# Attention of layer 0: three small matmuls per pair of rows trade places and one of them changes its PSUM bank

## The chip, the cores and the metric

The kernel runs on one core of one Trainium2 chip. The metric is the device time of one execution in microseconds (us). The engines are TensorE (PE in the profile), VectorE (DVE), ScalarE (ACT), GpSimd (POOL) and SyncE (SP, which only issues DMAs here).

## The reference, cut to what matters

The program has two layers on a picture of 256 x 256 positions with 128 channels. Layer 0, which the change touches, is an attention within each row of the picture, ahead of a residual addition:

```
xn = layernorm(groupnorm(x));  tri_bias = xn @ w_tri          # one bias per head, [h, m, n]
q = xn @ w_q / sqrt(32);  k = xn @ w_k;  v = xn @ w_v         # 4 heads of 32 channels
for each row i of 256:                                        # 256 positions m, n in a row
    scores = q[i] @ k[i].T + tri_bias + mask_bias[i, n]
    o[i] = softmax(scores over n) @ v[i]
x = x + (sigmoid(xn @ w_g + b_g) * o) @ w_o + b_o
```

Layer 1 is a convolution and a selective scan over windows in four directions, and takes about nine tenths of the time. The change doesn't touch it.

## The kernel before, in words

Channels lie on the 128 partitions and positions on the free axis. A first part normalises x and stores xn in HBM. Then the attention of layer 0 runs over 256 rows, two rows being a *pair* of 512 positions (class `Pair`, class `Row`). The order of all instructions is written out by hand (`tc.manual_schedule()`, the loop over `s` at L567): each engine carries out its own instructions in the order in which this loop issues them, and waits where its data or its buffer isn't ready. Layer 1 follows, with an order of its own.

One *step* s of the loop takes one row, and four rows are under way at once:

- `now` is row s: its scores in PSUM get their bias (`add`, L472, VectorE), their maximum (`peak`, L480, VectorE) and their exponential (`exps`, L488, ScalarE). That is done in two halves of two heads each.
- `nxt` is row s+1: `scores` (L462, TensorE).
- `mid` is row s-2: `turn` transposes its exponentials on TensorE (L516); `turn_out` copies them out of PSUM, one half on VectorE (L528), the other on ScalarE (L530).
- `old` is row s-3: `mix` multiplies with the values into `o_p` (L539, TensorE).
- At the end of a step the sums of row s-1 are inverted (L498, VectorE) and spread (`widen`, L503, GpSimd); GpSimd also prepares the bias of row s+2 (L449).

What is done once for a pair is spread over its two steps, s even and s odd. `ahead` is the next pair, `behind` the previous one, `done` the one before that:

- for `ahead`: `queries` (L364) and `queries_out` (L368), `keys` (L372) and `keys_out` (L376), `values` (L381) and `values_out` (L391); the matmuls are TensorE's, the copies out of PSUM ScalarE's;
- for `behind`: `gates` (L395, TensorE), `gates_out` (L399, VectorE) and the sigmoid in three passes of ScalarE (`logistic`, L131 to L133); `shares`, the transposes of the inverted sums (L409, TensorE), and `shares_out`, which multiplies them into the gate (L416, VectorE);
- for `done`: `gather`, gate times mixed values (L420, VectorE); `project`, the output projection (L424, TensorE); `project_out`, bias and residual (L427, VectorE); `store`, statistics for the next group norm (L432, VectorE) and the DMA to HBM (L433, SP).

PSUM has eight banks, and all of them are in use: four hold the scores, two the transposed exponentials (`aT_p`), one, `ps_o`, holds `o_p`, and one, the side bank (`side0`, tag "m"), is used by `g_p`, `q_p`, `y_p`, `k_p`, `rd_p` and `v_p` in this turn, once each in a pair. Each of the six has to wait until the one ahead of it has been read out.

The order within a step, with what stands in even or odd steps alone:

```
even: mix, add 0, peak 0, turn 0, exps(1 of 4), gather, turn_out 0, exps(3 of 4), gates, gates_out,
      add 1, turn 1, turn_out 1, peak 1, queries, queries_out, exps(4), scores, project,
      sigmoid, invert, widen
odd:  mix, add 0, peak 0, turn 0, exps(1 of 4), project_out, turn_out 0, exps(3 of 4), keys, keys_out,
      add 1, turn 1, turn_out 1, peak 1, shares, shares_out, exps(4), scores, values, values_out,
      store, invert, widen
```

Of the kernel before, what the change touches and what calls it, by code (L numbers as in the profile page):

```python
# [12 lines left out]
F32 = mybir.dt.float32  # L13
# [6 lines left out]
P = 128  # L20
# [47 lines left out]
def kernel(  # L68
# [60 lines left out]
    def logistic(e):  # L129

        nc.scalar.activation(e, e, AF.Exp, scale=-1.0)  # L131
        nc.scalar.activation(e, e, AF.Ln, bias=one)
        nc.scalar.activation(e, e, AF.Exp, scale=-1.0)  # L133
# [42 lines left out]
    for dh in range(2):  # L176
        for k in range(KD):
            o, back = k % 2, k // 2
# [82 lines left out]
    with tc.tile_pool(name="lnc", bufs=1) as cp, tc.tile_pool(  # L261
        name="lnx", bufs=3
    ) as xp, tc.tile_pool(name="lnt", bufs=3) as tp, tc.tile_pool(
        name="lnp", bufs=2, space=PSUM
# [47 lines left out]
    with tc.tile_pool(name="atc", bufs=1) as cp, tc.tile_pool(  # L312
        name="atx", bufs=7
    ) as xp, tc.tile_pool(name="att", bufs=3) as tp, tc.tile_pool(
        name="ats", bufs=8
    ) as wp, tc.tile_pool(name="atps", bufs=1, space=PSUM) as ps_s, tc.tile_pool(
        name="atpt", bufs=1, space=PSUM
    ) as ps_t, tc.tile_pool(name="atpm", bufs=1, space=PSUM) as ps_m, tc.tile_pool(
        name="atpo", bufs=1, space=PSUM
# [17 lines left out]
        def side0(name):  # L337
            return ps_m.tile([P, 512], F32, name=name, tag="m")

        class Pair:  # L340
# [79 lines left out]
                nc.vector.tensor_mul(self.og, self.o_p, self.gate)  # L420

            def project(self):
                self.y_p = side0("y_p")
                nc.tensor.matmul(self.y_p, wo, self.og, start=True, stop=True)  # L424

            def project_out(self):
# [8 lines left out]
        class Row:  # L435
# [96 lines left out]
            def mix(self):  # L532
                pair = self.pair
                if self.r == 0:
                    pair.o_p = ps_o.tile([P, 512], F32, name="o_p")
                for n in range(2):
                    for h in range(NH):
                        base = h * HC
                        nc.tensor.matmul(  # L539
                            pair.o_p[base : base + HC, self.row],  # L540
                            pair.vs[:, self.r, n, base : base + HC],
                            self.aT[h][:, n, :],
                            start=(n == 0),
                            stop=(n == 1),
                        )
# [4 lines left out]
        def pick(items, i):  # L550
            return items[i] if 0 <= i < len(items) else None

        with tc.manual_schedule():
            for pair in pairs[0:4]:
                pair.load()
            first = pairs[0]
            first.mask_bias()
            rows[0].bias()
            rows[1].bias()
            first.queries()  # L560
            first.queries_out()
            first.keys()
            first.keys_out()
            rows[0].scores()
            first.values()
            first.values_out()
            for s in range(n_rows + 4):  # L567
                sg, odd = divmod(s, 2)
                now, nxt, mid, old = (
                    pick(rows, s),  # L570
                    pick(rows, s + 1),
                    pick(rows, s - 2),
                    pick(rows, s - 3),
                )
                ahead, behind, done = (
                    pick(pairs, sg + 1),
                    pick(pairs, sg - 1),
                    pick(pairs, sg - 2),
                )
                if not odd:  # L580
                    if sg + 4 < n_pairs:
                        pairs[sg + 4].load()
                    if behind:
                        behind.load_residual()
                    if ahead:
                        ahead.mask_bias()
                if s + 2 < n_rows:
                    rows[s + 2].bias()
                if old:
                    old.mix()  # L590
                if now:
                    now.add(0)
                    now.peak(0)
                if mid:
                    mid.turn(0)
                if now:
                    now.exps(0, [0])
                if done:
                    if odd:
                        done.project_out()  # L600
                    else:
                        done.gather()
                if mid:
                    mid.turn_out(0)
                if now:
                    now.exps(0, [1, 2, 3])
                if odd and ahead:
                    ahead.keys()
                    ahead.keys_out()
                if not odd and behind:  # L610
                    behind.gates()
                    behind.gates_out()
                if now:
                    now.add(1)
                if mid:
                    mid.turn(1)
                    mid.turn_out(1)
                if now:
                    now.peak(1)
                if odd and behind:  # L620
                    behind.shares()
                    behind.shares_out()
                if not odd and ahead:
                    ahead.queries()
                    ahead.queries_out()
                if now:
                    now.exps(1, [0, 1, 2, 3])
                if nxt:
                    nxt.scores()
                if odd and ahead:  # L630
                    ahead.values()
                    ahead.values_out()
                if not odd and done:
                    done.project()
                if odd and done:
                    done.store()
                if not odd and behind:
                    logistic(behind.gate)
                if 0 <= s - 1 < n_rows:
                    rows[s - 1].invert()  # L640
                    rows[s - 1].widen()
# [778 lines left out]
```

## Time and profile before

| what | value |
|---|---|
| median of 3 runs (lowest, highest) | 24756.14 us (24755.36, 24756.92) |
| the profiled execution, and its span | 24756.32 us, 24754.5 us |
| mean granted TensorE clock in the whole span | 0.987 of full speed |
| attention of layer 0: first and last start of L472 | 543.3 us, 2720.6 us |
| busy in those 2177.3 us: PE, DVE, ACT, POOL | 1870.3, 1925.2, 1729.2, 1334.9 us |
| mean granted TensorE clock in them | 0.96 |

The profile gives, for each engine, the time in which it was busy with an instruction; the rest is waiting, and the trace says for each wait which instruction of which engine ended it. The matmuls' ends are modelled, and records of neighbouring instructions on one engine overlap a little, so the distance from one start to the next is shorter than the duration of a record. All numbers of the trace are from the one profiled execution.

### The profile page before, as it was taken

The page shows a single profiled execution, that of the slowest core. Times are in us where ns is not written, and L with a number is a line of the kernel's source. Part 1 is how long each engine was busy: PE and PEld are TensorE (multiplying, and loading weights), DVE is VectorE, ACT ScalarE, POOL GpSimd, SP SyncE. Part 2 cuts the span into 40 slices and gives each one's busy share as a digit, 9 for nine tenths or more (in the row PEclk, how much of TensorE's full clock was granted, in tenths as well). Part 3 has the DMA queues.
Part 4 walks back from the last instruction along what each step waited for, and adds up shares of the span by engine and source line. Part 5 has one row for each costly group of instructions (what it writes and reads, how often), then busy time and mean ns, then how long its engine had stood idle before and what let it go on. Part 6 is the DMA issues. An engine that isn't in the chain of part 4 may idle for free.

```text
span 24754.5 us, 429436 instructions
## 1 busy us (share of the span) xinstructions
PE 23738.4 (96%) x171020; PEld 17003.5 (69%) x171020; DVE 22137.9 (89%) x14740; ACT 18874.1 (76%) x35334; POOL 21878.7 (88%) x10062
## 2 busy tenths in 40 slices
PE   7888899999999999999999999999999999999999
PEld 2555577777777777777777777777777777777776
DVE  6888899999999999999999999999999999999998
ACT  5777777777777777777777777777777777777776
POOL 3666699999999999999999999999999999999999
PEclk9999999999999999999999999999999999999999
DMA  5222344444444444444444444444444444444444
GB/s 192 63 63 62 101 155 156 156 153 155 155 155 154 152 155 156 156 155 152 155 155 155 155 154 154 156 156 154 153 154 156 155 154 155 153 155 156 155 154 143
DMA packets 2000343, 3638.88 MB, mean 147 GB/s; under 512 B 1129584, under 2 KB 1131760, under 8 KB 1725824
## 3 DMA queue, kind: packets, MB, share of 16 engines
q1 hardware_dynamic: 1985616, 3602.35, 43.1%
q8 instruction: 1346, 22.05, 0.4%
q10 hardware_dynamic: 12720, 9.07, 0.1%
q14 instruction: 661, 5.41, 0.1%
HBM read 3467.33 MB, written 143.65 MB: 146 GB/s over the span
## 4 chain that ended last, share of the span: by engine, by line
PE 82%; DVE 8%; ACT 6%; issue 2%; POOL 1%; DMA 0%; ACTq 0%; SPq 0%; DVEq 0%; POOLq 0%
PE b_p L1173 31%; PE y_p L1206 28%; DVE h L1189 5%; PE cv_p L762 5%; PE dt_p L1011 4%; ACT at L488 2%; PE xd_p L942 2%; PE dut_p L1045 2%; PE in_p L717 1%; PE o_p L878 1%; PE y_p L1064 1%; PE z_p L796 1%; PE u_p L915 1%; PE sc L462 1%; POOL h L1195 1%
## 5 line engine op out<-in xcount | busy, mean ns | idle before, releaser
L1195 POOL TENSOR_TENSOR h<-h,cc 128x1024 f32<-128x1024 f32 x8192 | 19182.8, 2369 | 1524.1 <-DVE h L1189 1514.1
L1189 DVE TENSOR_TENSOR_SCAN h<-da,b_p 128x1024 f32<-128x1024 f32 x8192 | 18346.7, 2274 | 2068.7 <-PE b_p L1173 2011.5
L1160 ACT ACTIVATE da<-dt,am 128x508 f32<-128x508 f32 x16384 | 10663.9, 708 | 1910.4 <-DVE h L1189 1899.3
L1173 PE MATMUL b_p<-diag,dut 64*128 64x256 f32 x65536 | 9139.4, 401 | 388.2 <-DVE h L1189 386.8
L1206 PE MATMUL y_p<-ident,h 128*128 128x128 f32 x65536 | 8168.1, 278 | 7.7 <-POOL h L1195 7.6
L1206 PEld LDWEIGHTS y_p<-ident,h 128*128 128x128 f32 x65536 | 7207.2, 142 | 1406.7 <-issue 1062.0
L1173 PEld LDWEIGHTS b_p<-diag,dut 64*128 64x128 f32 x65536 | 5700.1, 186 | 3303.5 <-issue 1848.3
L734 ACT ACTIVATE tap<-xin,wtap 128x512 f32<-128x512 f32 x2048 | 1519.6, 742 | 0.5
L762 PE MATMUL cv_p<-ident,tap 128*128 128x128 f32 x9216 | 1446.1, 280 | 31.1 <-ACT tap L734 27.1
L1021 ACT ACTIVATE sp<-dt_p 128x512 f32<-128x512 f32 x1024 | 610.3, 596 | 1079.2 <-PE dt_p L1011 1078.4
L1034 POOL TENSOR_TENSOR du<-dt,u 128x512 f32<-128x512 f32 x1024 | 1308.6, 1278 | 59.9 <-DMA z<-bt 57.0
L762 PEld LDWEIGHTS cv_p<-ident,tap 128*128 128x128 f32 x9216 | 1037.9, 141 | 390.4 <-issue 204.9
L1151 ACT ACTIVATE da<-ident 128x16 f32<-128x16 f32 x1536 | 349.3, 227 | 1202.2 <-DVE h L1189 1202.1
L488 ACT ACTIVATE at<-at,nmax 128x256 f32<-128x256 f32 x2048 | 1019.2, 501 | 240.0 <-DVE nmax L480 240.0
L449 POOL TENSOR_TENSOR tm<-trib,mb 128x2048 f32<-128x2048 f32 x256 | 1166.3, 4556 | 10.7
L1011 PE MATMUL dt_p<-xd,wdt 9*128 9x512 f32 x2048 | 1149.6, 641 | 2.5 <-DVE dt L1027 2.2
L503 POOL COPY wide<-rden 128x256 f32<-128x256 f32 x256 | 101.6, 397 | 828.5 <-DVE rden L498 826.6
L1054 ACT COPY dut<-dut_p 128x512 f32<-128x512 f32 x1024 | 589.0, 575 | 256.9 <-PE dut_p L1045 245.2
L1022 ACT ACTIVATE sp<-sp,one 128x512 f32<-128x512 f32 x1024 | 739.6, 722 | 33.7
L1027 DVE SCALAR_TENSOR_TENSOR dt<-sp,dt_p 128x512 f32<-128x512 f32 x1024 | 677.9, 662 | 15.4 <-DMA z<-bt 11.5
L516 PEld LDWEIGHTS aT_p<-ident,at 128*128 128x128 f32 x4096 | 450.8, 141 | 343.0 <-issue 142.6
L472 DVE TENSOR_TENSOR at<-sc,tm 128x1024 f32<-128x1024 f32 x512 | 614.4, 1200 | 57.7 <-POOL wide L503 30.3
(132 smaller groups left out, 16405.1 us busy)
## 6 DMA issues: line engine op xcount, KB each, us to landing
cc<-c_d SPq DMA_DIRECT2D x2048, 1024.0 KB
diag<-z SPq DMA_DIRECT2D x1024, 1024.0 KB
xt<-in_x_dram SPq DMA_DIRECT2D x16, 2048.0 KB
xt<-in_x_dram SPq DMA_DIRECT2D x32, 1024.0 KB
xn_d<-xn SPq DMA_DIRECT2D x32, 1024.0 KB
xn<-xn_d SPq DMA_DIRECT2D x128, 256.0 KB
mb<-in_mask_dram SPq DMA_DIRECT2D x128, 256.0 KB
xr<-in_x_dram SPq DMA_DIRECT2D x128, 256.0 KB
```

The lines of the kernel that those rows point to most:

```text
L449: nc.gpsimd.tensor_add(self.tm, trib.rearrange("p h m n -> p (h m) n"), self.pair.mb[:, self.row].unsqueeze(1).to_broadcast([P, 2 * NH, IMG]),
L488: nc.scalar.activation(self.at[hp][:, j, :], self.at[hp][:, j, :], AF.Exp, bias=self.nmax[hp][:, j : j + 1], accum_out=self.den[:, 2 * hp ...
L734: nc.scalar.activation(scaled.rearrange("p s (y x) -> p s y x", x=WIN), self.xin[:, dh] .rearrange("p y f x -> p (y f) x")[:, 2 * dy : 2 * ...
L762: nc.tensor.matmul(cv_p[:, s], now[:, s], ident, start=(tap == 0 and s == 0), stop=(tap == 8 and s == GS - 1), is_transpose=True, skip_gro ...
L1011: nc.tensor.matmul(token_order(self.dt_p), wdt[rows, self.o, dh * P : (dh + 1) * P], token_blocks(self.xd[rows]), start=True, stop=True,)
L1022: nc.scalar.activation(sp, sp, AF.Ln, bias=one)
L1034: nc.gpsimd.tensor_mul(token_blocks(du), token_order(self.dt[back][dh]), token_blocks(self.u[:, dh]),)
L1160: nc.scalar.activation(da[:, :, j, lo:hi], dt[:, :, lo:hi], AF.Exp, scale=am[:, a0 : a0 + 1])
L1173: nc.tensor.matmul(b_p[:, s, :, h * 64 : (h + 1) * 64].rearrange("p n t -> p t n"), job.dut[self.back][rows, p, h, self.dh * P : (self.dh ...
L1189: nc.vector.tensor_tensor_scan(out=out_, data0=d0, data1=d1, initial=0.0, op0=ALU.mult, op1=ALU.add)
L1195: nc.gpsimd.tensor_mul(self.h, self.h, cc.rearrange("p n s t -> p s n t"))
L1206: nc.tensor.matmul(job.y_p[:, 2 * p + s, self.dh * P : (self.dh + 1) * P], self.h[:, s, j], ident, start=(first and s == 0 and j == 0), st ...
```

## The change

Three things change in the order, and one buffer. The projection's result `y_p` is written into the bank of `o_p` instead of the side bank, and `project` with `project_out` stands in the even step behind `queries_out`; before, `project` was at the end of the even step and `project_out` in the odd one. `keys` and `keys_out` stand at the end of the even step, behind the scores and ahead of the sigmoid; before, they were in the odd step ahead of `add 1`. The matmuls of `shares` take the place of the keys in the odd step, ahead of the second turn and of the values; `shares_out` stays. The turn of the side bank becomes `g_p`, `q_p`, `k_p`, `rd_p`, `v_p`.

```diff
             def project(self):
-                self.y_p = side0("y_p")
+
+                self.y_p = ps_o.tile([P, 512], F32, name="y_p", tag="o")
                 nc.tensor.matmul(self.y_p, wo, self.og, start=True, stop=True)
...
             def mix(self):
                 pair = self.pair
                 if self.r == 0:
-                    pair.o_p = ps_o.tile([P, 512], F32, name="o_p")
+                    pair.o_p = ps_o.tile([P, 512], F32, name="o_p", tag="o")
...
                 if now:
                     now.exps(0, [0])
-                if done:
-                    if odd:
-                        done.project_out()
-                    else:
-                        done.gather()
+                if done and not odd:
+                    done.gather()
                 if mid:
                     mid.turn_out(0)
                 if now:
                     now.exps(0, [1, 2, 3])
-                if odd and ahead:
-                    ahead.keys()
-                    ahead.keys_out()
+                if odd and behind:
+                    behind.shares()
                 if not odd and behind:
                     behind.gates()
                     behind.gates_out()
...
                 if now:
                     now.peak(1)
                 if odd and behind:
-                    behind.shares()
                     behind.shares_out()
                 if not odd and ahead:
                     ahead.queries()
                     ahead.queries_out()
+                if not odd and done:
+                    done.project()
+                    done.project_out()
                 if now:
                     now.exps(1, [0, 1, 2, 3])
...
                 if odd and ahead:
                     ahead.values()
                     ahead.values_out()
-                if not odd and done:
-                    done.project()
+                if not odd and ahead:
+                    ahead.keys()
+                    ahead.keys_out()
                 if odd and done:
                     done.store()
```

## The prediction, made before the result was known

> **What bounds the kernel now.** I read the page first: one core, 24754.5 us of span inside an execution of 24756.3. The edit touches only the attention of layer 0, so I cut that stage out: the first score addition (L472) starts at 543.3 us, the last at 2720.6. Those are 255 steps (one image row each), 8.54 us a step, **17.08 us a pair of rows**. Then the view by windows, first over the steady part, then over two single pairs (from the L472 that opens an even step to the next such):
>
> ```profile
> core 0: us, PE busy (x) PEld busy (x) DVE busy (x) ACT busy (x) POOL busy (x), PEclk, DMA share, GB/s
> 700.00:2700.00 2000.00, 1721.32 (x13597) 1032.85 (x13596) 1773.05 (x2227) 1591.90 (x4921) 1227.22 (x586) 0.96 0.21 62
> ...
> 1514.98:1531.42 16.44, 14.03 (x118) 8.34 (x117) 15.05 (x20) 13.55 (x43) 10.48 (x5) 1.00 0.19 66
> ```
>
> No engine is full, VectorE (DVE) comes nearest with 89%, and it does the same 15.05 us of work in a pair of 16.44. So I asked what DVE, TensorE (PE) and ScalarE wait for (columns: total us, times, longest):
>
> ```profile
> DVE gate L416 <- PE rd_p L409: 155.2, 117, 1.6
> DVE at L472 <- POOL wide L503: 28.4, 45, 1.0
> DVE gate L399 <- PE g_p L395: 26.9, 48, 0.6
> ...
> PE rd_p L409 <- ACT ks L376: 162.8, 117, 1.4
> PE k_p L372 <- DVE xr L427: 72.9, 117, 0.6
> PE aT_p L516 <- ACT aT L530: 39.7, 117, 0.3
> ```
>
> One wait stands out and comes once in each of the 117 pairs: DVE's product with the shares waits for the transposes rd_p, and these wait for ScalarE's copy of the keys, because k_p and rd_p use the one side bank in turn. k_p in turn waited for DVE to empty y_p out of that bank. The chain of waits over one pair shows what it hangs on:
>
> ```profile
> 1522.29 2.08 ACT at L488 x8
> 1524.37 0.53 ACT gate L131
> ...
> 1526.31 0.49 ACT at L488 x2
> 1526.81 0.47 ACT aT L530
> 1527.28 1.49 ACT at L488 x6
> 1528.77 0.48 ACT ks L376
> 1529.24 0.14 issue
> 1529.38 0.63 PE rd_p L409 x4
> 1530.01 1.08 PE sc L462 x16
> ```
>
> ScalarE runs exponentials and the sigmoid without a gap, the keys' copy is last in that row, and everything on PE and DVE stands behind it. Last, the granted clock in two odd steps:
>
> ```profile
> 1494.00:1496.00 2.00, 1.07 (x8) 0.79 0.81 221
> 1496.00:1498.00 2.00, 2.00 (x17) 0.50 0.02 8
> ...
> 1528.00:1530.00 2.00, 0.62 (x8) 1.00 0.66 235
> ```
>
> (after the PE busy time: clock, DMA share, GB/s.) PE is nearly idle for that wait, and in some pairs the clock then falls to 0.50 for about 4 us: scores take 2.09 us there instead of 1.15, and the next L472 and L399 wait (the 45 and 48 cases above, some 40% of 117). A pair without a drop takes 16.44, the mean is 17.08: the drop costs **0.64 us a pair** on average.
>
> **What the Trainium skill says.** "TensorE: Matmul & The Clock Gate", Part 1, says that an idle window of about 3.4 us takes the array to half its clock and a busy one restores it, the windows running freely. The trace agrees in kind: 0.50 after a gap, only in some pairs. The worst 3.4 us of the fast pair (1525.98 to 1529.39) still hold 1.67 us of PE work, 49%, so a half-idle window seems to be enough here. "PSUM — Partial Sum Buffer", Engine vs sequencer instructions: ScalarE, VectorE and GpSimd take their queues strictly in order and matmuls complete in program order. The trace agrees: k_p was computed by 1526.4, yet its copy starts at 1528.66, after the exponentials issued ahead of it. The same page, PSUM bank collisions, asks that a bank be guarded as a whole: y_p in the bank of o_p must wait for gather (L420) to have read o_p, which its data need anyway.
>
> **The change part by part.** I lay out one pair from t=0 at the even step's first L472 (1514.98 in the trace), with start-to-start distances from there: L472 1.21 and 1.14, peak L480 1.14, gather 0.60, turn copy 0.60, gates 0.67, L427 0.66, shares product 0.61, statistics 0.60, reciprocal 0.10. Counts per pair 4, 4, 1, 4, 1, 1, 1, 1, 2: that is 15.00 us without waits. Taken from the other side, 16.44 less 1.36 for L416's gap and 0.12 for L399's is **14.96 us**, which I use.
>
> *Removed on DVE:* the wait before L416. Work removed or added: none on any engine; every matmul and copy stays, they change places.
>
> *Even step, DVE:* L472 0, peak 1.21, gather 2.35, copy 2.95, gates 3.55 to 3.67, L472 4.34, copy 5.47, peak 6.07, then the moved project_out (L427) at 7.19, reciprocal 7.85, end 7.96. *PE:* mix 0.68, turn 1.68, gates 2.6, second turn 3.68 (after DVE's copy), queries 4.61, **project 5.57 to 6.62** (1.05), scores to 7.71, keys 8.68 (0.97). Project waits for gather, over at 3.0: nothing. project_out wants y_p at 6.7 and comes at 7.19: slack 0.5, cost nothing. The scores are 1.05 later behind project, but the next L472 is 0.66 later too: 7.71 against 7.96. *ScalarE:* queries_out ends at 6.2, so the side bank is free long before keys; exponentials 7.31 to 9.29 (behind the peak), keys_out to 9.77 (k_p was ready at 8.7), sigmoid to 11.72. In front of the sigmoid keys_out delays it by 0.48; gone from the odd step it gives that back. The sigmoid's result is wanted by the shares product at 13.8, 2 us later.
>
> *Odd step, PE:* mix at 8.68 takes the o bank, free since project_out ended near 7.93; turn to 10.61; **shares at once**, since keys_out freed the bank at 9.8 and GpSimd's wide copy comes some 0.6 after the reciprocal (8.6): 10.61 to 11.17, 3 us ahead of their use. Second turn: first half to 11.75; second half waits for ScalarE's L530, 0.96 after the sigmoid (12.68), to 13.4. Scores 14.5, values 14.55. *DVE:* L472 7.96, peak 9.17, copy 10.31, L472 10.91, copy 12.06 (its transposes end at 11.8), peak 12.66, shares product 13.8, statistics, reciprocal, end **15.0**. Values wait for that product (14.49): nothing. The next gates reach DVE near 18.55, DVE stands there at 18.5 to 18.6; I keep the 0.12 that the fast pair shows.
>
> So the pair becomes **15.08 us**. The second longest loop is peak, exponentials 2.08, keys_out 0.48, sigmoid 1.89, exponential and copy 0.96, half a turn 0.7, scores 1.08, values 1.09, mix 1.00, turn 1.02, gates 0.88, then DVE 0.75+1.13+0.60+1.14: 14.8, hardly shorter. That, and not PE's 14.03 of work, is what is late next.
>
> *Queues:* GpSimd has 10.5 us in 15.1. SP stores a pair after L427 and issues the next loads behind it; both come about 1.7 us earlier, for inputs needed pairs later: nothing. *Clock:* PE now idles about 1.0 us in one place (11.75 to 12.75); its worst 3.4 us are 70% busy, against 49% before. I take the drop as gone.
>
> Sum against the profiled execution: 127.5 pairs x (17.08 - 15.08) = 255 us, of which 82 is the clock; 24756 - 255 = **24501 us**, and the median of the runs is the same within 0.2. Bounds: without any wait 14.96, 270 us, 24486; a few us more at the stage's ends, 24480. With 0.25 of small waits more per pair, 24533. The trace doesn't show project between queries and scores; its cost lies between nothing and 1.05 less the 0.5 of slack, and I take nothing.
>
> **The rivals.** (B) *The clock still drops* as often as now. For: a gap of 1 us remains. Against: 70% busy. Price 0.64 a pair: 15.72, **24583**. (C) *A new wait on DVE for y_p:* queries and project stand in one row behind the turn; if they come 1.5 us later than laid out, DVE waits 1.0 in each pair: 16.08, **24629**. Against: PE has no wait in this stretch today. (D) *Slower:* keys_out now stands ahead of the sigmoid, so a late k_p stops ScalarE, with it the odd step's turn, scores and the next L472. It has 0.6 of slack (8.7 against 9.29); it decides once k_p comes after about 11.7, 3 us late (then the pair passes 17.47). That takes a half clock all through the even step, PE's 5 us from the second turn to keys becoming 10: k_p at 13.7, pair 19.5, **25065**. Against: the even step's clock is 1.00 and PE hardly waits there. (E) *It doesn't do what it says,* a release of the shared o bank serialising the pair anew as y_p did: no change, 24756.
>
> **How the numbers follow.** A 0.75, B 0.11, C 0.08, D 0.04, E 0.02. A measurement of this kernel can tell about 0.2%, 50 us, from no change. Faster: A, B and C, 0.94; same 0.02; slower 0.04. Range: A with its bounds and B, 24480 to 24590.
>
> **What would show it.** Right: L416 no longer waits for rd_p; L472 starts every 15.1 us per two; DVE near 99% in the stage, last additions near 2466 us; clock about 1.0. Wrong: a wait of L427 for y_p (C), of L376 for k_p (D), a clock of 0.96 or less (B), or PE's mix waiting for L427 (E).

## The result, and the profile after

The changed kernel takes **24494.94 us** (median of 4 runs, 24492.64 to 24498.18) against 24756.53 us, a ratio of 0.9894 with a 95% interval of 0.9877 to 0.9912. That is 262 us less; the prediction was 24501. The profiled execution has a span of 24490.9 us. In this listing the lines from `project` on have moved by one: L427 is now L428, L472 is L473, L488 is L489, L516 is L517, L530 is L531.

The score additions now run from 542.7 to 2456.5 us, 255 steps in 1913.8 us: 15.01 us a pair, before 17.08. So the stage gave 263.5 us, and the whole span is 263.6 us shorter: nothing else moved. The view by windows of the changed kernel, over the steady part and over one pair (columns as before):

```profile
700.00:2450.00 1750.00, 1598.54 (x13523) 968.34 (x13522) 1741.87 (x2217) 1565.00 (x4899) 1219.21 (x582) 1.00 0.24 70
...
1499.97:1514.98 15.01, 13.72 (x118) 8.30 (x118) 14.94 (x21) 13.43 (x44) 10.48 (x5) 1.00 0.24 71
```

VectorE is busy for 1741.87 of 1750 us, which is 99.5% against 89% before, and the clock is 1.00 against 0.96. The work per pair is nearly as it was (VectorE 14.94 us against 15.05, TensorE 13.72 against 14.03). Who waits in the changed kernel (columns: total us, times, longest):

```profile
ACT at L489 <- DVE nmax L481: 156.7, 233, 1.0
PE aT_p L517 <- ACT aT L531: 125.7, 117, 1.1
...
PE v_p L381 <- DVE gate L416: 0.5, 2, 0.2
```

In this stretch no wait of VectorE is left in the list; before, over as many pairs (117), the product with the shares alone stood for 155 us. TensorE keeps one wait per pair, for ScalarE's copy that frees a bank of the turn. The timeline of TensorE and VectorE shows the pair as it now runs (start, duration, engine, line, what; in brackets a wait ahead of it):

```profile
1505.43 1.02 PE L425 MATMUL y_p<-og,wo 128*128 128x512 f32 x2
...
1507.46 1.12 PE L372 MATMUL k_p<-xn,wk 128*128 128x512 f32 x2
...
1510.45 0.60 PE L409 MATMUL rd_p<-ident,wide 128*128 128x128 f32 x4
...
1512.69 0.65 PE L517 MATMUL aT_p<-ident,at 128*128 128x128 f32 x4 [1.07 <-ACT aT L531]
```

```profile
1507.07 0.74 DVE L428 SCALAR_TENSOR_TENSOR xr<-y_p,bo,xr 128x512 f32<-128x512 f32 x1
...
1513.68 0.68 DVE L416 TENSOR_TENSOR gate<-gate,rd_p 128x512 f32<-128x512 f32 x1
```

Counted from the even step's first L473 at 1499.97, project starts at 5.46 (laid out: 5.57), L428 at 7.10 (7.19), keys at 7.49 (7.71), shares at 10.48 (10.61), the second half of the turn at 12.72 (12.75), the shares product at 13.71 (13.8). rd_p is ready 2.6 us before VectorE comes for it.

### The profile page after: what moved, and what is told of

The parts are those of the page before. It is cut to its first block, busy times and chain, and to the rows that moved or that the text cites. A ratio compares the mean times of both kernels' runs of the same rounds, so it can differ in the third digit from the quotient of the medians.

```text
span 24490.9 us, 429433 instructions
## 1 busy us (share of the span) xinstructions
PE 23614.5 (96%) x171020; PEld 16936.4 (69%) x171020; DVE 22114.2 (90%) x14740; ACT 18849.5 (77%) x35334; POOL 21879.7 (89%) x10062
## 4 chain that ended last, share of the span: by engine, by line
PE 80%; DVE 14%; ACT 3%; issue 2%; POOL 1%; DMA 0%; ACTq 0%; DVEq 0%; SPq 0%; POOLq 0%
PE b_p L1173 31%; PE y_p L1206 28%; DVE h L1189 5%; PE cv_p L762 5%; PE dt_p L1011 4%; DVE nmax L481 2%; DVE at L473 2%; PE xd_p L942 2%; PE dut_p L1045 2%; PE in_p L717 1%; PE o_p L878 1%; DVE aT L529 1%; PE y_p L1064 1%; PE z_p L796 1%; PE u_p L915 1%
## 5 line engine op out<-in xcount | busy, mean ns | idle before, releaser
L489 ACT ACTIVATE at<-at,nmax 128x256 f32<-128x256 f32 x2048 | 1018.3, 500 | 172.6 <-DVE nmax L481 172.6
L517 PE MATMUL aT_p<-ident,at 128*128 128x128 f32 x4096 | 587.0, 281 | 155.0 <-ACT aT L531 136.8
L517 PEld LDWEIGHTS aT_p<-ident,at 128*128 128x128 f32 x4096 | 436.3, 141 | 414.4 <-ACT aT L531 166.9
L1045 PE MATMUL dut_p<-ident,du 128*128 128x128 f32 x4096 | 644.2, 280 | 3.5 <-DVE dt L1027 2.3
```

The source lines that it names most:

```text
L517: nc.tensor.transpose(aT_p[:, n, mc * P : (mc + 1) * P], self.at[hp][:, 2 * hh + mc, n * P : (n + 1) * P], ident,)
L1045: nc.tensor.transpose(self.dut_p[:, h * DI + dh * P : h * DI + (dh + 1) * P], self.du[back][dh][:, (2 * h + p) * P : (2 * h + p + 1) * P], ...
```

## The experiments

All times are medians; "before" is the kernel before, measured beside each group on the same chip (24757.84 us for e1 to e4, 24754.72 for e5 to e8, 24755.42 for e9 and e10); across the groups it differs by 3 us. A pair's length is the distance from one even step's first score addition to the next in the trace.

**e4: the clock alone.** The kernel before, with more work for TensorE in its gap.

```diff
-            def turn(self, hp):
+            def turn(self, hp, again=0):
...
+                    for n, mc in again * [(0, 0), (0, 1), (1, 0), (1, 1)] if hh else []:
+                        nc.tensor.transpose(
+                            aT_p[:, n, mc * P : (mc + 1) * P],
+                            self.at[hp][:, 2 * hh + mc, n * P : (n + 1) * P],
+                            ident,
+                        )
...
-                    mid.turn(1)
+                    mid.turn(1, 2 * odd)
```

> The kernel before with one addition: in odd steps the second half of the second turn is carried out three times instead of once (eight transposes more, 1.1 us of PE, the same values into the same bank), so PE works in the gap in which it waits for the keys' copy. They end about when ScalarE comes to read that bank, so the pair's chain should not be lengthened. Theory (the half clock comes from PE's gap and costs 0.64 us a pair): clock 1.00 in the stage, every pair 16.4 to 16.6, 24675 to 24700 us. Rival (the clock falls for another reason, the transfers or the work of the other engines, which are the same here): clock 0.96 as before, pair 17.1 or more, 24756 us or more.

Measured: 24678.46 us, ratio 0.9968 (0.9956 to 0.9980). The kernel does more and is 79 us faster. Its windows and its waits:

```profile
700.00:2450.00 1750.00, 1586.86 (x13211) 981.23 (x13210) 1601.78 (x2023) 1441.37 (x4472) 1114.59 (x534) 1.00 0.23 65
```

```profile
DVE gate L416 <- PE rd_p L409: 136.0, 107, 1.6
```

The clock is 1.00, the wait for rd_p is still there with 1.27 us in each of the 107 pairs, and the pairs are 16.44 us nearly throughout. Nothing else in the kernel differs, the transfers and the other engines' work are the same; so the half clock comes from TensorE's gap; its price is 79 us where the prediction had 82.

**e1: the projection and its bank alone.**

```diff
-                self.y_p = side0("y_p")
+                self.y_p = ps_o.tile([P, 512], F32, name="y_p", tag="o")
...
-                if done:
-                    if odd:
-                        done.project_out()
-                    else:
-                        done.gather()
+                if done and not odd:
+                    done.gather()
...
+                if not odd and done:
+                    done.project()
+                    done.project_out()
...
-                if not odd and done:
-                    done.project()
```

> The kernel before with the first part of the change alone: y_p in the bank of o_p, project and project_out behind queries_out in the even step; keys and shares stay in the odd step. Theory (the pair hangs on ScalarE's queue: rd_p waits for the keys' copy, which stands behind exponentials, sigmoid and exponentials): that queue is not touched, k_p merely comes earlier and waits longer to be copied. The copy still ends 14.2 us after the even step's first L472, rd_p comes at 15.0, DVE stands ready at 13.8 and waits 1.2 to 1.3 us for it in each pair; pair 16.4 to 17.1, 24670 to 24760 us (the spread is the clock, which has a gap as large as before). Rival (what held the side bank was y_p, so its own bank is the gain): no wait for rd_p, pair near 15.0, below 24560 us.

Measured: 24864.28 us, ratio 1.0043 (1.0026 to 1.0060): slower, outside both expectations. The chain did stay as the theory had it: where the clock is full, a stretch of it repeats after 16.44 us and rd_p still waits for the keys' copy (134.9 us). What I had sized wrong is the clock. The view by windows, cut into stretches of 3.413 us that follow one another (TensorE busy, clock, DMA share, GB/s), shows how it goes; first the kernel before, then e1:

```profile
1525.86:1529.28 3.42, 1.78 (x10) 1.00 0.65 226
1529.28:1532.69 3.41, 3.31 (x40) 1.00 0.23 81
...
1542.93:1546.34 3.41, 1.68 (x13) 1.00 0.92 242
1546.34:1549.76 3.42, 3.42 (x23) 0.50 0.11 41
```

```profile
1515.73:1519.14 3.41, 1.79 (x10) 1.00 0.61 174
1519.14:1522.55 3.41, 2.90 (x20) 0.50 0.00 0
1522.55:1525.97 3.42, 3.42 (x25) 0.50 0.00 0
1525.97:1529.38 3.41, 3.41 (x27) 1.00 0.00 0
```

With this one grid laid over the whole stage, the clock is either full or half within each window. In the kernel before (700 to 2700 us) it fell 47 times, each time for one window, after windows with 1.67 to 1.70 us of TensorE work; no window with 1.77 or more was followed by a fall. In e1 (700 to 2800 us, some 118 pairs) it fell 87 times, after windows with 1.36 to 1.82 us; 29 falls lasted two windows, those where the first half-clock window held at most 2.92 us of work, and it came back after every one with 3.03 or more. The grid agrees with what the Trainium skill has in "TensorE: Matmul & The Clock Gate", Part 1 (a free-running window of 3413 ns); but the page lets the clock fall after an idle window, and here windows that were 40 to 53% busy were enough. e1 spends 116 windows at half clock where the kernel before spent 47, in about as many pairs.

**e10: e1 with the gap filled.** The edit of e4, in e1.

> e1 (projection and its bank alone) with TensorE's gap filled as in e4: in odd steps the second half of the second turn is carried out three times. Theory (the bank and the place of the projection change nothing in the chain, and all that e1 lost against the kernel before is the half clock, which its gap brings in half of the pairs and for twice as long): clock 1.00, every pair 16.44, the same time as e4, 24670 to 24690 us. Rival (y_p in the bank of o_p costs a wait of its own, mix for project_out): 24780 us or more.

Measured: 24676.07 us, ratio 0.9968 (0.9956 to 0.9980), the same as e4, and the clock is 1.00. So the bank and the place of the projection alone are worth nothing in the chain, and what e1 loses is clock: 24864 less 24676 is 188 us, 1.5 us a pair.

**e7: the keys alone.**

```diff
-                if odd and ahead:
-                    ahead.keys()
-                    ahead.keys_out()
...
                 if not odd and done:
                     done.project()
+                if not odd and ahead:
+                    ahead.keys()
+                    ahead.keys_out()
```

> The kernel before with the move of the keys alone: keys and keys_out at the end of the even step, y_p still ahead of them in the side bank, emptied in the odd step. This is the mechanism of rival D: a late k_p in front of the sigmoid on ScalarE. k_p waits on TensorE for project_out, at 10.4 us after the even step's first L472, and everything behind it on TensorE with it; ScalarE reaches keys_out at 9.3 and stands until 11.5. Sigmoid, the odd step's turn, scores and additions all come 2 us later. Theory: pair 17.8 to 18.2, and with the clock's drops up to 0.6 more, 24850 to 24980 us. Rival (an early place of the keys is a gain by itself, since rd_p no longer waits for the keys' copy): below 24700 us.

Measured: 24972.86 us, ratio 1.0087 (1.0072 to 1.0102). The waits say how:

```profile
DVE aT L528 <- PE aT_p L516: 354.6, 93, 5.1
...
PE k_p L372 <- DVE xr L427: 236.1, 93, 2.6
ACT ks L376 <- PE k_p L372: 232.7, 93, 3.2
```

k_p waits 2.5 us for y_p to leave the side bank, which `project_out` empties in the odd step only, and ScalarE stands 2.5 us at the keys' copy, in each of 93 pairs. VectorE then waits 3.8 us for the turn that stands behind the keys on TensorE; the wait for rd_p is gone, and that is no gain at all. A pair is 18.8 us on average (1750 / 93), the clock 0.93. This is the mechanism of rival D, a late k_p in front of the sigmoid. The change has two guards against it: y_p is in another bank, and `project_out` stands in the even step, ahead of the keys.

The clock of e7 falls on a grid of the same length, 80 times from 700 to 2800 us, after windows with 0.87 to 1.57 us of TensorE work. But it kept full speed after five windows with 1.58 to 1.61 us, less than the 1.67 after which it fell in the kernel before (columns as under e1):

```profile
1429.66:1433.07 3.41, 1.61 (x14) 1.00 0.23 81
1433.07:1436.48 3.41, 2.50 (x27) 1.00 0.82 223
```

So the busy time in the profile doesn't give one exact level for all kernels; what else counts isn't shown.

**e2: the bank of y_p undone.**

```diff
-                self.y_p = ps_o.tile([P, 512], F32, name="y_p", tag="o")
+                self.y_p = side0("y_p")
```

> The changed kernel with the bank of y_p undone: all moves stay, y_p is in the side bank between q_p and k_p. Theory: project then waits for ScalarE's copy of q_p (6.2 us after the even step's first L472) and ends at 7.3 in place of 6.6, project_out on DVE waits 0.2, keys wait for project_out but ScalarE reaches their copy only at 9.3, so the pair grows by 0.2 to 0.4 us: 24520 to 24546 us. Rival (sharing the one side bank six ways restores the old chain, the bank is what counts): 1 us or more per pair, 24620 us or more.

Measured: 24615.87 us, ratio 0.9943 (0.9928 to 0.9958); pair 15.96. The size is nearly the rival's, the mechanism isn't: VectorE never waits for rd_p.

```profile
PE y_p L425 <- ACT qs L368: 75.6, 110, 0.7
PE v_p L381 <- DVE gate L416: 64.9, 109, 0.8
...
DVE xr L428 <- PE y_p L425: 33.0, 110, 0.3
DVE at L473 <- PE sc L463: 30.2, 108, 0.3
```

Project waits 0.69 for ScalarE's copy of q_p, as laid out. I had let only project_out pay for it; but scores, keys, mix and the odd step's turn stand in line behind project on TensorE, and VectorE pays at L428, at the odd L473 and at the turn's copy (its start 1509.22 is 0.2 late). With y_p back, 121 of the 262 us are lost. Rival D does not come back with it: k_p is late for ScalarE by only 0.3 us a pair (35.1 us in 110 waits), where e7 had 2.5. So the early `project_out` is nearly enough to keep D away without the other bank; the other bank with a late `project_out` was not run.

**e3: the shares undone.** `behind.shares()` goes back to the place directly ahead of `behind.shares_out()`.

> The changed kernel with the shares' transposes back behind the second turn, directly ahead of shares_out. Theory: PE does the second half of that turn only when ScalarE's copy frees the bank (12.7 us after the even step's first L472), so rd_p is there at about 14.0 to 14.1 and DVE, ready at 13.7, waits 0.3; scores, values, mix, turn and gates all come 0.5 us later and DVE waits some 0.2 again at the gates: pair 15.4 to 15.5, 24545 to 24560 us with the clock still near 1.0. Rival 1 (with the keys early the place of the shares is worth nothing): 24495 us. Rival 2 (the PE gap grows and the half clock comes back, as before the change): 0.6 us more, 24620 to 24640 us.

Measured: 24538.14 us, ratio 0.9911 (0.9896 to 0.9926); pair 15.33, clock 1.00. It is 7 us less than the range expected. VectorE's wait is there again, small:

```profile
DVE gate L416 <- PE rd_p L409: 19.8, 110, 0.2
```

The theory holds in kind, with 0.32 us a pair in place of 0.4 to 0.5: the product starts 0.26 us later behind the peak than in the changed kernel, and the gates 0.10 us later behind the turn's copy. The place of the shares is worth 43 us.

**e5 and e6: what sets the pair now.** In e5 the line of L433 stands twice. In e6:

```diff
-                nc.vector.bn_stats(stats[:, self.pr, :], self.xr)
+                nc.vector.bn_stats(stats[:, self.pr, :], self.xr[:, 0:16])
```

> The changed kernel with the statistics of a pair (L433, VectorE, 0.60 us from start to start) carried out twice. Theory (after the change VectorE works without a wait and sets the pair's length): all of it shows, pair 15.0 + 0.6 = 15.6 us, 127.5 pairs: 24495 + 77 = 24572 us. Rival (the loop through ScalarE and TensorE sets the length, VectorE merely keeps up): the 0.6 hides at least in part, 24495 to 24530 us.

> The changed kernel with the statistics taken over 16 of the 512 positions (what is left out: layer 1's group norm gets its mean and variance from those alone). It takes some 0.45 to 0.5 us of VectorE's work per pair away. Theory (VectorE first, and close behind it the loop peak, exponentials, keys_out, sigmoid, second turn, scores, values, mix, turn, gates, that I put at 14.8 us): pair 14.8, about 24470 us. Rival (that loop has far more room than I think): pair 14.5, 24432 to 24440 us.

Measured, e5: 24590.19 us, ratio 0.9933 (0.9918 to 0.9948), 95 us more than the changed kernel; pair 15.73. All of it shows. It is more than the 77 expected because the second of the two starts 0.72 us after the first and not 0.60. e6: 24489.15 us, ratio 0.9892 (0.9876 to 0.9909), only 6 us less than the changed kernel, too little to tell apart by the intervals, where about 25 were expected; pair 14.96, which the trace does tell apart from 15.01. Here VectorE waits again (34.9 us in 115 waits of L399 for g_p), and the chain of waits passes through ScalarE and TensorE:

```profile
1508.47 2.08 ACT at L489 x8
1510.55 0.47 ACT ks L376
...
1513.46 0.48 ACT aT L531
1513.94 0.04 issue
1513.98 0.66 PE aT_p L517 x4
1514.64 1.09 PE sc L463 x14
```

That is the second loop of the prediction, with the length of 14.96 where I had added up 14.8. VectorE sets the pair of the changed kernel, but the other loop is only 0.05 us shorter.

**e8: less work on VectorE.** (The gate's lower limit of -40 is left out in e8 and e9.)

```diff
             def gates_out(self):
                 self.gate = tp.tile([P, 512], F32, name="gate")
-                nc.vector.tensor_scalar(self.gate, self.g_p, bg, FLOOR, ALU.add, ALU.max)
+                nc.scalar.activation(self.gate, self.g_p, AF.Exp, bias=nbg, scale=-1.0)
...
-                if not odd and ahead:
-                    ahead.queries()
-                    ahead.queries_out()
                 if not odd and done:
                     done.project()
                     done.project_out()
+                if not odd and ahead:
+                    ahead.queries()
+                    ahead.queries_out()
```

Not shown: `nbg` is the gate's bias with its sign changed, and the two other passes of the sigmoid stay in their place.

> The changed kernel with less on VectorE: gates_out (L399) is dropped, and ScalarE's first pass of the sigmoid reads g_p out of PSUM with the bias in the activation, at the place of gates_out; the lower limit of -40 on the gate falls away. As g_p now holds the side bank until about 5.5 us, project stands ahead of queries. VectorE loses 0.67 us a pair, ScalarE's work stays the same, but one pass of 0.63 moves from behind the exponentials into a stretch where it waited for the peak. Theory: pair 14.35 to 14.5, 24412 to 24431 us. Rival (queries 1 us later delay the scores behind them, and VectorE waits for these in the odd step): 24480 us or more.

Measured: 24530.44 us, ratio 0.9909 (0.9894 to 0.9924): 35 us more than the changed kernel, the rival. VectorE has 0.67 us less to do and waits for more than that, 0.71 us a pair:

```profile
DVE at L479 <- PE sc L469: 81.9, 115, 1.1
```

**e9: the same with another order.**

```diff
                 if mid:
                     mid.turn(0)
+                if odd and ahead:
+                    ahead.keys()
+                    ahead.keys_out()
...
                     mid.turn_out(0)
+                if not odd and ahead:
+                    ahead.queries()
+                    ahead.queries_out()
...
+                if mid:
+                    mid.turn(1, (0,))
+                if odd and behind:
+                    behind.shares()
                 if mid:
-                    mid.turn(1)
+                    mid.turn(1, (1,))
                     mid.turn_out(1)
...
                 if not odd and behind:
-                    logistic(behind.gate)
+                    behind.gates()
+                    behind.sigmoid()
```

The lines of the keys, the queries, the gates and `now.add(1)` in their old places are taken out (not shown); `sigmoid` has the three passes of ScalarE, the first as in e8.

> As e8 the gate without VectorE (ScalarE's first pass of the sigmoid reads g_p out of PSUM, no lower limit on the gate), but with an order that takes e8's late queries away: in the even step queries stand between the two turns, where TensorE waits for the bank of the turn, with queries_out behind turn_out 0; gates stand behind the scores, directly ahead of the sigmoid; keys go to the odd step behind the first turn, with their copy ahead of the odd exponentials; shares stand between the halves of the second turn. Theory (VectorE's 14.96 less 0.67, and the loop through ScalarE and TensorE loses the gates, since the even step's L399 is gone from it): pair 14.3 to 14.5, 24405 to 24430 us. Rival (TensorE, 13.7 us of work per pair in strict order, is now the bound with its waits): 14.9 or more, 24480 us or more.

Measured: **24397.87 us**, ratio 0.9855 (0.9839 to 0.9872), below the interval of the changed kernel and 7 us below the range expected; pair 14.25. Its windows (700 to 2350 us):

```profile
700.00:2350.00 1650.00, 1582.22 (x13422) 955.82 (x13424) 1642.10 (x2084) 1570.43 (x4861) 1214.54 (x578) 1.00 0.25 74
```

VectorE is busy for 1642.10 of 1650 us and waits for nobody. Here its work came off together with the second loop, and the pair fell by 0.76 us; TensorE and ScalarE now stand at 96 and 95%, and the rival, TensorE as the bound, did not come.

## Why the prediction was right

- **What bounds it.** Right. The wait of L416 was the end of a chain through ScalarE's queue and the side bank; it is gone and nothing took its place on VectorE. e4 and e10 show that neither a full clock nor the projection's move touches that chain.
- **The clock.** Right in kind and size: 82 us predicted, 79 in e4. The worst 3.4 us of the changed pair (1511.30 to 1514.70) hold 2.25 us of TensorE work, 66%, well above every window after which the clock fell (1.82 us at most, in e1); I had 70%. A drop in the kernel before lasts 3.41 us and not about 4. That a half-busy window is enough was a guess that came out: the pair from which I read the 49% kept its clock, and only the grid under e1 shows it.
- **The layout.** The starts named above came up to 0.22 us earlier than laid out, and the slack of L428 for y_p held.
- **The sum.** 15.08 a pair predicted, 15.01 measured; that is 9 us over 127.5 pairs, and the profiled execution (24492.64) lies 8 below the 24501. Two errors of opposite sign stand behind it: 14.96 was slightly short for VectorE alone, where the plain sum of its distances, 15.00, was the better figure, and the 0.12 us for the gates was hardly paid. That the first hides a part of the second is luck.
- **The second loop** was mis-sized: 14.8 against 14.96 (e6). In the trace of e6 the peak takes 1.24 us to its result where I had 1.14, and the sigmoid and the values are 0.05 and 0.04 longer. That did no harm, since the loop is still not longer than VectorE's; that is luck too, as another 0.1 us would have shown.
- **The rivals.** B didn't come (clock 1.00), nor C, nor E: L428 and mix hardly wait. D's mechanism is real: e7 has it, at 18.8 us a pair. The early `project_out` nearly keeps it away by itself: e2, with y_p in the side bank, shows only 0.3 us of it. The prediction didn't say that the place of the keys depends on the place of the projection.

How the 262 us fall to the parts can't be added up from single edits: the projection alone loses 106 us, the keys alone lose 218, and with both in place, y_p's own bank is worth 121 and the place of the shares 43. Only the clock term is a figure of its own, 79.

## What to carry to other kernels

When several engines are 80 to 90% busy and none is full, it can help not to look for the busiest one: take one period, find the wait that comes exactly once in it, and follow who owns the buffer behind that wait. Lay the new order out on all queues with start-to-start distances, and count what stands in line behind each instruction that comes later, not only who reads its result. A part of a reordering can cost time by itself and gain together with the others, so judge it whole, and test parts only to learn what depends on what.

## What the runs showed of the hardware that was not expected

- TensorE's clock is decided anew every 3.413 us on a grid that held through the whole stage, and it falls after windows that are far from idle: after 1.67 to 1.70 us of work in the kernel before and up to 1.82 in e1, about half, though TensorE's longest wait in these two was 1.4 us. The level isn't the same in all kernels: e7 kept the clock after 1.58 us. To come back it took a half-clock window with about 3 us of work (2.92 not enough, 3.03 enough in e1; 2.91 and 2.96 in e7).
- More work can be faster: eight transposes more per pair took 79 us off (e4).
- Two statistics in a row over the same input into the same place start 0.72 us apart (e5). In the same run, 100 statistics in a row over inputs and into places of their own (L255) take 59.99 us, 0.60 each. Whether the input or the place makes the difference isn't shown.
